# A four-image layer of state-space branches, attention and expert networks: row transfers stop beside one image's gates, one image's norm closes up, and a small table takes more of its operands from PSUM

## The chip, the cores and the metric

The kernel runs on one core of a Trainium2 chip. A core has five engines that each work through a queue of their own: TensorE (PE, matrix products), VectorE (DVE, elementwise work on tensors, scans and reductions), ScalarE (ACT, functions of one tensor), GpSimd (POOL, elementwise work and transfers by index) and SyncE (SP, transfers). An engine starts an instruction when the one before it is through and what it waits for has been signalled. Working memory is SBUF, with 128 partitions; PE writes its results to PSUM, a smaller memory of eight banks, which DVE and ACT read and write too. The metric is the device time of one launch in microseconds (us).

## The reference

The input x has the shape (4, 256, 32, 32): four images, 256 channels, 1024 positions. What is computed, cut to its order:

```python
x = x + conv_layer(_ln_c(x))          # the "metaformer" layer
t = tokens(x)                         # 4096 rows of 256 channels
t = t + experts(_ln_t(t))             # top 2 of 8 networks for each row

# conv_layer:
xn = layernorm(xs)                    # over channels
xm = mamba of each of 4 channel groups (xn) + skip * xn
g  = sigmoid(conv1d(conv1d(xm)))      # a gate of each group and position
xg = g * xm
R  = conv1d(depthwise3(xg)) + xg      # 3 taps along the positions, then channels mixed
xm2 = conv1d(depthwise3([xs, R])) + xs
out = mix([depthwise3(xm2), attention(xm2)])   # 8 heads, softmax over 1024 positions
... layernorm, gelu, 3 x 3 depthwise, layernorm, projection
```

The Mamba branch runs a recurrence of 16 states for each of 128 inner channels: `h = dA_t * h + dBu_t`, then `y_t = sum(h * C_t)`. The input of the layer is itself normalised over channels (`_ln_c`), so two layer norms follow one another; the kernel folds them into one mean, one variance and two roots. The expert layer sends each row to two of eight networks of width 1024.

## The kernel before

**Order.** The order of the instructions in every engine's queue is written out by hand: work is put into the queues in the order in which Python issues it (`tc.manual_schedule` over all five engines). Generators issue a few instructions and then yield a number of *ticks*. `beat()` (line 1571 and on) makes one tick: it steps every generator that is due, in the order in which they were started. The main loop, from about line 1605, puts one scan step into the queues and then calls `beat()`, so in a tick the scan's instructions come first and the rest follows.

**Scan.** An image b (0 to 3) has eight *parts*: four branches by two halves of 512 positions. A part has 16 scan steps. A step has, for 128x512 values each, the decay on ACT (line 732), the inflow on DVE (742), the recurrence as one scan instruction on DVE (753), the multiply with C on POOL (761, written dA<-hs,cs), the spread of B on PE (724) and the sum over states on PE (771). Around a part's start POOL also makes dt (682, 686), and at its end z (779).

**Beside and between the scans.** In the first half of image b's scan runs `convolutions(b-1)`: the gates (ACT 958 and 963, POOL 971) and the 3-tap depthwise convolutions `depthwise3` (the first tap on ACT, line 457; the two others on DVE, line 462). The products d4r<-xm come after them, with taps of the same function. After part 3 the scan's loop is interrupted for `attention(b-1)`: scores on PE (1140), exponentials on ACT (1150), pairs of them added on DVE (1200), the product with v on PE (1190). When its marker "attended" is set, the scan goes on with part 4, and whatever else is still running shares the ticks of the scan.

**The norm.** `normalised(b)` (from line 514) makes the normed input of image b. For image 2 it runs as an entry of its own, started together with attention of image 0: sums over the two channel chunks, centring, squares (POOL), column means (PE), the roots r1 and r2 (ACT, lines 419 and 420), then by chunk: xl = xn * r1 (POOL, 570), xn * r2 (DVE, 572), a transfer of xl to XL in DRAM, a scale and shift (POOL, 575), and `own_taps` (from 583): a first tap on ACT (586), two on DVE (593), a transfer to XD. The squares of image 2 are added up over the chunks into one operand (`one_chunk`), kept in the buffers of r1 and r2.

**Routing and row transfers.** When an image is finished, `sent_off` runs `experts.dispatch(b)`: it norms the rows, finds two experts for each, and writes each row into its expert's region of XS. That takes 16 transfers by index on POOL for each image (line 1975), each behind a small memset (1974). For image 0 two ticks lie between them. `dispatch(0)` runs in the scan of image 3, parts 0 and 1, beside `convolutions(2)`; it was started earlier, so in a tick its transfer is put in ahead of the gate's multiply.

**The expert tiles.** `tiles()` starts with the last part of the scan. It takes tiles of 256 rows, each of one expert. Which expert a tile has and where its rows begin is worked out in tables, one for each series of tiles: `series` calls `table` (line 2041 and on), some 22 DVE instructions on 128x8 or 128x64 values. The first table (series 0, in the last scan at about 1405 us) gets a PSUM bank, `first_table`, and keeps some of its operands there. The later tables are all in SBUF. After the scan of image 3 and its convolutions and attention, nearly all that is left is products of the expert tiles on PE (2364, 2397).

Of the kernel before, what the change touches and what calls it, by code (L numbers as in the profile page):

```python
# [11 lines left out]
ALU = mybir.AluOpType  # L12
AX = mybir.AxisListType

P = 128
# [4 lines left out]
HALF = 512  # L20
# [58 lines left out]
def network(  # L79
# [71 lines left out]
    with tc.tile_pool(name="w_conv", bufs=1) as wp, tc.tile_pool(  # L151
# [371 lines left out]
        def normalised(b):  # L523


            place_xn(b)
            xn = XN[b]

            def part(c, h):
                return xn[:, c, ds(LEFT + h * HALF, HALF)]  # L530

            yield 4

            def centre(h, mean):
                for c in range(NC2):
                    nc.vector.tensor_tensor(part(c, h), part(c, h), mean, ALU.subtract)

            r1, r2 = a4(f"r1_{b}"), a4(f"r2_{b}")
            one_chunk = b == 2
            if one_chunk:  # L540
                for h in range(2):
                    nc.gpsimd.tensor_tensor(r1[:, half(h)], part(0, h), part(1, h), ALU.add)
                yield 2
            yield from in_turn(
                range(2), lambda h: column_mean(
                    f"mean_{b}_{h}",
                    [r1[:, half(h)]] if one_chunk else [part(c, h) for c in range(NC2)],
                ),
                centre,
            )  # L550
            for h in range(2):
                if one_chunk:
                    sq = [v[:, half(h)] for v in (r1, r2)]
                else:
                    sq = [a2(f"sq_{b}_{h}_{c}") for c in range(NC2)]
                for c in range(NC2):
                    nc.gpsimd.tensor_tensor(sq[c], part(c, h), part(c, h), ALU.mult)
                if one_chunk:
                    nc.gpsimd.tensor_tensor(sq[0], sq[0], sq.pop(), ALU.add)
                    yield 1  # L560
                yield 1
                var = column_mean(f"var_{b}_{h}", sq)
                yield 2
                root(r1[:, half(h)], var, eps6)
                yield 1
                root(r2[:, half(h)], var, eps11, scale=1.0 + 1e-5)
                yield 1
            for c in range(NC2):
                xl = a4(f"xl_{b}_{c}")
                nc.gpsimd.tensor_tensor(xl, xn[:, c, LEFT:], r1, ALU.mult)  # L570
                yield 2
                nc.vector.tensor_tensor(xn[:, c, LEFT:], xn[:, c, LEFT:], r2, ALU.mult)
                yield 1
                nc.sync.dma_start(XL[b][:, c, :], xl)
                nc.gpsimd.tensor_scalar(
                    xn[:, c, LEFT:], xn[:, c, LEFT:], col("norm_w", c), col("norm_b", c),
                    ALU.mult, ALU.add,
                )
                yield 1
                if b in XD and b < B - 1:  # L580
                    yield from own_taps(b, c, xl)
# [330 lines left out]
        def convolutions(b):  # L912
# [54 lines left out]

            def gating():
                yield from in_turn(range(NC2), gate, keep)
                for c in range(NC2):  # L970
                    nc.gpsimd.tensor_tensor(
                        xm[:, c, 1 : N + 1], gs[c], xm[:, c, 1 : N + 1], ALU.mult
                    )
                    yield 1
                for c in range(NC2):
                    yield from depthwise3(d[1], c, xm, c, "rdw_w", c, col("rdw_b", c))

            def mixed(at, r):
                co, h = at
# [366 lines left out]
        def sent_off(b):  # L1346

            xc = XC.pop(b)
            beside = b < B - 2
            if b == B - 2:  # L1350
                yield 6

            def centre(h, mean):
                for c in range(NC2):
                    nc.vector.tensor_tensor(
                        xc[:, c, half(h)], xc[:, c, half(h)], mean, ALU.subtract
                    )

            pace(b, PACE["norm"])
            xr = a8(f"xr_{b}")  # L1360
            nc.sync.dma_start(xr, x[b].rearrange("(c p) n -> p c n", p=P))
            yield from in_turn(
                range(2),
                lambda h: column_mean(f"mean_{b}_{h}", [xc[:, c, half(h)] for c in range(NC2)]),
                centre,
            )
            yield from inverse_deviation(f"fin_{b}", xc, b == B - 1, b == 1)

            def residual(at, r):
                co, h = at  # L1370
                inner = xr[:, co, half(h)]
                if beside:
                    nc.scalar.activation(inner, r, AF.Identity, bias=prb[:, co : co + 1])
                else:
                    nc.vector.scalar_tensor_tensor(
                        inner, r, prb[:, co : co + 1], inner, ALU.add, ALU.add
                    )

            yield from in_turn(
                CO_H, lambda at: product(  # L1380
                    f"pr_{b}_{at[0]}_{at[1]}", projT_s, at[0],
                    [xc[:, ci, half(at[1])] for ci in range(NC2)],
                    xr[:, at[0], half(at[1])] if beside else None,
                ), residual,
            )
            T["projected", b] = True
            pace(b, PACE["routing"])
            for ticks in experts.dispatch(
                b, xr, act8.tile(experts.XR, F32, tag="a8", name=f"XR_{b}"), root,
                log_exp, lambda: T.get("exps"),  # L1390
            ):
                if experts.counted == b:
                    pace(b, PACE["rows"])
                yield ticks
            T["sent", b] = True
            pace(b, 1)
# [259 lines left out]
class Experts:  # L1656
# [155 lines left out]
    def s1(self, name):  # L1812
        return self.m0.tile([P, self.NT, 1], F32, tag=name, name=name)

    def dispatch(self, b, X1, XR, root, log_exp, recent):

        nc, tc, psum, m0, NT = self.nc, self.tc, self.psum, self.m0, self.NT
        s1, s3, all_e = self.s1, self.s3, self.all_e
# [152 lines left out]
        apart = self.apart  # L1971
        for j in range(2):
            for t in range(NT):
                nc.gpsimd.memset(apart, 0.0)
                ins = nc.gpsimd.indirect_dma_start(  # L1975
                    out=self.XS[:, :],
                    out_offset=bass.IndirectOffsetOnAxis(ap=to[:, j, t : t + 1], axis=0),
                    in_=XR[:, t, :], in_offset=None,
                )
                for other in self.sent + self.read:  # L1980
                    tc.declare_no_dep(ins.ins, other.ins, reason="no two share a row")
                self.sent.append(ins)
                if b == self.B - 2 and recent():
                    self.follow(ins, [recent()], "one after the other")
                if b == self.B - 1 and j == 0:
                    self.blank_end(t)
                yield 2 if b in (0, 2) or b == 1 and t % 2 else 1
# [53 lines left out]
    def table(self, temp, keep, name, n, ntile, which, done=None, kinds=NE, bank=None):  # L2041
# [16 lines left out]
        S = [P, n, kinds]  # L2058
        past = temp(f"past_{name}", S)
        nc.vector.tensor_tensor(past, which, ends.to_broadcast(S), ALU.is_ge)  # L2060
        if bank is None:
            inside = temp(f"inside_{name}", S)
        else:
            inside = bank[:, ds(3 * kinds, n * kinds)].rearrange("p (n e) -> p n e", e=kinds)
        nc.vector.tensor_tensor(inside, which, starts.to_broadcast(S), ALU.is_ge)
        nc.vector.tensor_tensor(inside, inside, past, ALU.subtract)
        expert = keep(f"expert_{name}", [P, n, 1])
        nc.vector.tensor_reduce(expert, past, AX.X, ALU.add)
        nc.vector.tensor_scalar(expert, expert, float(kinds - 1), None, ALU.min)
        if kinds > NE:  # L2070
            second = temp(f"second_{name}", [P, n, 1])
            nc.vector.tensor_scalar(
# [1 line left out]
            )  # L2074
            nc.vector.tensor_tensor(expert, expert, second, ALU.add)

        nc.vector.tensor_tensor(which, which, starts.to_broadcast(S), ALU.subtract)
        if done is not None:
            nc.vector.tensor_tensor(which, which, done.to_broadcast(S), ALU.add)
        nc.vector.tensor_scalar(  # L2080
            which, which, float(self.T), float(-self.SPARE), ALU.mult, ALU.add
        )
        for k in range(0, kinds, NE):
            nc.vector.tensor_tensor(
                which[:, :, k : k + NE], which[:, :, k : k + NE],
                self.region[:, 0:1, :].to_broadcast([P, n, NE]), ALU.add,
            )
        nc.vector.tensor_tensor(which, which, inside, ALU.mult)
        first = temp(f"first_{name}", [P, n, 1])
        nc.vector.tensor_reduce(first, which, AX.X, ALU.add)  # L2090
        table = self.m0.tile([P, 2, n], mybir.dt.int32, name=f"table_{name}")
        nc.vector.tensor_copy(table[:, 0, :], expert.rearrange("p n a -> p (n a)"))
        nc.vector.tensor_scalar(
# [458 lines left out]
```

## Time and profile before

| | us |
|---|---|
| three runs | 2158.35, 2160.07, 2161.26 |
| their median | 2160.07 |
| profiled execution | 2160.25 |
| its span, first to last instruction | 2158.5 |
| outside the span | 1.75 |
| PE busy | 1921.5 (89%) |
| DVE busy | 1539.0 (71%) |
| ACT busy | 1212.5 (56%) |
| POOL busy | 1052.9 (49%) |
| mean granted TensorE clock | 0.963 of full speed |

Stages of the profiled execution, in us from its start: scan of image 0 to about 260; first half of image 1's scan with convolutions of image 0 to about 435; attention of image 0 from 438 to 530; the second half of image 1's scan from there; attention of image 1 from about 793; the gates of image 2 and the last three row transfers of image 0 from 1084 to 1111; the first table from 1404 to 1412; the end of the last scan to 1437; expert tiles, with the rest of image 3, to the end.

A line of an engine's timeline reads: start in us, length in us, engine, line of the kernel, operation, output<-inputs by the program's names, the size of output and inputs, the number of instructions put together; in square brackets the idle time of the engine just before, and what ended it. Where one line stands for several instructions (x2 and more), its length covers them all.

### The profile page before, as it was taken

What the parts mean: (1) busy time and instruction counts of PE and PEld (TensorE: products, weight loads), DVE (VectorE), ACT (ScalarE), POOL (GpSimd) and SP (SyncE); (2) the same over time, 40 slices, a digit from 0 to 9 for tenths busy, and PEclk for the clock granted to TensorE, in tenths of its full rate; (3) what the DMA queues carried; (4) which work ended last, traced back from release to release, by engine and by line L of the source; (5) the groups of instructions that cost most, each with busy time, mean ns of one, the idle gap of its engine ahead of it and who ended that gap; (6) DMA issues with size and microseconds to landing.
All of it is one profiled execution on the core that took longest, in us unless ns stands there. A gap on an engine that the chain in (4) does not pass through costs nothing. (4 is left out here: it accounts for less than half of the span.)

```text
span 2158.5 us, 28179 instructions
## 1 busy us (share of the span) xinstructions
PE 1921.5 (89%) x8682; PEld 866.5 (40%) x8682; DVE 1539.0 (71%) x2253; ACT 1212.5 (56%) x2274; POOL 1052.9 (49%) x935
## 2 busy tenths in 40 slices
PE   6778778999887999988789999769999989999996
PEld 2112112322211232223123223226743768888885
DVE  3999999876999989789889898986265345221121
ACT  4665657678676667677466876625267423222221
POOL 0787887731887850376878016752031012422131
PEclk8888999999999999998999999999999999999998
DMA  3665544311454431053734203445230166877764
GB/s 99 152 161 127 125 122 102 90 41 50 105 117 122 94 85 40 17 133 98 187 87 108 80 6 98 109 162 146 81 92 23 47 198 172 233 230 189 212 185 131
DMA packets 157087, 251.40 MB, mean 116 GB/s; under 512 B 34740, under 2 KB 101332, under 8 KB 156664
## 3 DMA queue, kind: packets, MB, share of 16 engines
q1 hardware_dynamic: 136560, 223.47, 38.2%
q0 software_dynamic: 12720, 17.32, 4.1%
q10 hardware_dynamic: 7640, 8.65, 1.3%
q8 instruction: 72, 1.18, 0.2%
q14 instruction: 95, 0.78, 0.1%
HBM read 137.22 MB, written 36.62 MB: 81 GB/s over the span
## 5 line engine op out<-in xcount | busy, mean ns | idle before, releaser
L761 POOL TENSOR_TENSOR dA<-hs,cs 128x512 f32<-128x512 f32 x512 | 684.0, 1345 | 374.7 <-DVE hs L753 246.7
L732 ACT ACTIVATE dA<-dts,A 128x512 f32<-128x512 f32 x512 | 359.0, 718 | 152.6 <-DMA dts<-dt 68.8
L771 PE MATMUL yp<-dA,quads 128*32 128x512 f32 x1024 | 284.4, 631 | 87.5 <-POOL dA L761 72.8
L2382 POOL DMA_INDIRECT Y<-ys,dest x68 | 109.6, 1612 | 425.4 <-DVE ys L2375 418.4
L1150 ACT ACTIVATE e<-st 128x512 f32<-128x512 f32 x512 | 263.6, 605 | 86.8 <-PE st L1140 81.6
L2369 ACT ACTIVATE hs<-h,b 128x256 f32<-128x256 f32 (+1 forms) x256 | 110.2, 479 | 345.6 <-PE h L2364 241.3
L742 DVE TENSOR_TENSOR dBu<-dts,bs 128x512 f32<-128x512 f32 x384 | 259.8, 677 | 48.9 <-PE bs L724 14.5
L753 DVE TENSOR_TENSOR_SCAN hs<-dA,last,dBu 128x512 f32<-128x512 f32 x192 | 243.7, 1269 | 2.9 <-PE yp L771 1.1
L2397 PE MATMUL y<-w,hs 128*128 128x256 f32 (+1 forms) x1088 | 243.3, 382 | 0.7 <-issue 0.4
L2364 PE MATMUL h<-xT,w 128*128 128x256 f32 (+1 forms) x1024 | 239.6, 390 | 0.8 <-DVE xT L2327 0.8
L753 DVE TENSOR_TENSOR_SCAN hs<-dA,dBu 128x512 f32<-128x512 f32 x192 | 231.9, 1208 | 1.9 <-PE av L1162 1.3
L1200 DVE TENSOR_TENSOR e<-e,e 128x512 f32<-128x512 f32 x256 | 171.0, 729 | 74.7 <-ACT e L1150 45.7
L2397 PEld LDWEIGHTS y<-w,hs 128*128 128x128 f32 (+1 forms) x1088 | 197.2, 188 | 37.7 <-issue 9.8
L2364 PEld LDWEIGHTS h<-xT,w 128*128 128x128 f32 x1024 | 195.3, 192 | 41.9 <-issue 8.3
L2327 DVE COPY xT<-xp 128x512 f32<-128x512 f32 (+1 forms) x36 | 23.3, 647 | 246.2 <-PE xp L2323 245.9
L724 PE MATMUL bs<-u,xpwT_s 128*32 128x512 f32 x1024 | 157.4, 651 | 39.7 <-DVE hs L753 15.0
L1140 PE MATMUL st<-qk 32*128 32x512 f32 x1024 | 174.4, 638 | 1.3 <-DVE hs L753 1.2
L771 PEld LDWEIGHTS yp<-dA,quads 128*32 128x32 f32 x1024 | 50.6, 112 | 297.7 <-POOL dA L761 196.4
L1190 PE MATMUL av<-e,v 128*32 128x512 f32 x1024 | 138.6, 604 | 0.0
L1975 POOL DMA_INDIRECT XS<-XR,to x64 | 65.6, 1025 | 92.3 <-ACT e L1150 53.9
L1140 PEld LDWEIGHTS st<-qk 32*128 32x128 f32 x1024 | 60.1, 183 | 115.7 <-issue 87.1
L742 DVE TENSOR_TENSOR bs<-dts,bs 128x512 f32<-128x512 f32 x128 | 86.2, 673 | 0.9 <-DMA dts<-dt 0.9
(374 smaller groups left out, 2637.3 us busy)
## 6 DMA issues: line engine op xcount, KB each, us to landing
dts<-dt SPq DMA_DIRECT2D x512, 128.0 KB
w<-in_W_dram SPq DMA_DIRECT2D x124, 512.0 KB
cs<-cd SPq DMA_DIRECT2D x512, 64.0 KB
xs<-XS SPq DMA_DIRECT2D x32, 260.0 KB
xd<-xn SPq DMA_DIRECT2D x64, 128.0 KB
xn<-in_x_dram SPq DMA_DIRECT2D x8, 512.0 KB
XL<-xl SPq DMA_DIRECT2D x8, 512.0 KB
xl<-XL SPq DMA_DIRECT2D x4, 1024.0 KB
```

The source lines that it names most:

```text
L724: nc.tensor.matmul(bs[r], xpwT_s[:, n, s : s + 1].to_broadcast([P, 32]), T[b, n, "u"][:, half(h)], start=True, stop=True,)
L732: nc.scalar.activation(dA, T[b, n, h, "dts", g][:, 0, :], AF.Exp, scale=A[:, g, n, q : q + 1])
L742: nc.vector.tensor_tensor(dBu, T[b, n, h, "dts", g][:, 1, :], T[b, n, h, "bs", q], ALU.mult)
L753: nc.vector.tensor_tensor_scan(hs, T[b, n, h, "dA", i], dBu, 0.0 if h == 0 else last, ALU.mult, ALU.add)
L761: nc.gpsimd.tensor_tensor(dA, hs, T[b, n, h, "cs", q], ALU.mult)
L771: nc.tensor.matmul(T[b, n, h, "yp"][ts(g, 32)], quads, T[b, n, h, "dA", q * GD + g], start=False, stop=(q == GS - 1),)
L1140: nc.tensor.matmul(sts[i], k[r, ts(kt, P)], q[r, half(h)], start=True, stop=not shifted)
L1150: ins = nc.scalar.activation(es[i], sts[i], AF.Exp, scale=1.0 / HD**0.5)
L1190: nc.tensor.matmul(accs[0][ts(i, HD)], v8[:, kt, ts(4 * g + i, HD)], es[i], start=(kt == 0), stop=(kt == NK - 1),)
L1200: nc.vector.tensor_tensor(first[i], first[i], es[i], ALU.add)
L2364: nc.tensor.matmul(hp[:, i, :], w1(c, k0 + i), xT[:, c, :], start=(c == 0), stop=(c == NC2 - 1))
L2397: nc.tensor.matmul(yp[ts(k % parts, n), ts(t % 2, C)], hidden(k)[:, ds(t * P, n)], w2(k), start=(k < parts), stop=(k >= NHC - parts),)
```

## The change

The change has three parts.

- `normalised`: the squares and the two roots become small functions. For image 2 alone the order is new: squares of half 0; a tick later squares of half 1 and the variance of half 0; then a root in each tick, with the variance of half 1 in the tick of its first root. That makes 6 ticks, where each half had 6 before. The other images keep their order.
- `convolutions` and `dispatch`: a marker `gating` is set from the first gate multiply until the two depthwise convolutions behind the gates are through (2 + 2 × 3 = 8 ticks), in images 0 to 2. `dispatch` yields a tick at a time while it is set, ahead of each transfer. Only `dispatch(0)` beside the gates of image 2 meets the marker.
- `table`: with a bank, the count of each tile's expert (`last`), the first row (`first`), the comparison with starts (`within`) and the products (`tell`) are in PSUM; `inside`, which was there, is in SBUF. Only the first table has a bank.

```diff
@@ normalised(b)
-            for h in range(2):
+            def squares(h):
                 if one_chunk:
                     sq = [v[:, half(h)] for v in (r1, r2)]
...
                 if one_chunk:
                     nc.gpsimd.tensor_tensor(sq[0], sq[0], sq.pop(), ALU.add)
-                    yield 1
-                yield 1
-                var = column_mean(f"var_{b}_{h}", sq)
-                yield 2
+                return sq
+
+            def roots(h, var):
                 root(r1[:, half(h)], var, eps6)
                 yield 1
                 root(r2[:, half(h)], var, eps11, scale=1.0 + 1e-5)
                 yield 1
+
+            if one_chunk:
+                sq = squares(0)
+                yield 1
+                sq, var = squares(1), column_mean(f"var_{b}_0", sq)
+                yield 1
+                yield from roots(0, var)
+                yield from roots(1, column_mean(f"var_{b}_1", sq))
+            else:
...
@@ convolutions(b), gating()
                 yield from in_turn(range(NC2), gate, keep)
+                T["gating",] = beside
                 for c in range(NC2):
...
                     yield from depthwise3(d[1], c, xm, c, "rdw_w", c, col("rdw_b", c))
+                T["gating",] = False
@@ dispatch
         for j in range(2):
             for t in range(NT):
+                while busy():
+                    yield 1
                 nc.gpsimd.memset(apart, 0.0)
@@ table
+        inside = temp(f"inside_{name}", S)
         if bank is None:
-            inside = temp(f"inside_{name}", S)
+            within, tell = inside, which
         else:
-            inside = bank[:, ds(3 * kinds, n * kinds)].rearrange("p (n e) -> p n e", e=kinds)
-        nc.vector.tensor_tensor(inside, which, starts.to_broadcast(S), ALU.is_ge)
-        nc.vector.tensor_tensor(inside, inside, past, ALU.subtract)
+            at = iter(range(3 * kinds + 2 * n, HALF, n * kinds))
+            within, tell = (
+                bank[:, ds(next(at), n * kinds)].rearrange("p (n e) -> p n e", e=kinds)
+                for _ in range(2)
+            )
+        nc.vector.tensor_tensor(within, which, starts.to_broadcast(S), ALU.is_ge)
+        nc.vector.tensor_tensor(inside, within, past, ALU.subtract)
         expert = keep(f"expert_{name}", [P, n, 1])
-        nc.vector.tensor_reduce(expert, past, AX.X, ALU.add)
-        nc.vector.tensor_scalar(expert, expert, float(kinds - 1), None, ALU.min)
+        if bank is None:
+            last, first = expert, temp(f"first_{name}", [P, n, 1])
+        else:
+            last, first = (
+                bank[:, ds(3 * kinds + k * n, n)].rearrange("p (n a) -> p n a", a=1)
+                for k in range(2)
+            )
+        nc.vector.tensor_reduce(last, past, AX.X, ALU.add)
+        nc.vector.tensor_scalar(expert, last, float(kinds - 1), None, ALU.min)
...
-        nc.vector.tensor_tensor(which, which, starts.to_broadcast(S), ALU.subtract)
+        nc.vector.tensor_tensor(tell, which, starts.to_broadcast(S), ALU.subtract)
...
-        nc.vector.tensor_reduce(first, which, AX.X, ALU.add)
+        nc.vector.tensor_reduce(first, tell, AX.X, ALU.add)
```

More of the change, by code (lines that the diff above doesn't have):

```diff
@@ L567, in normalised @@
                 yield 1
+            if one_chunk:
[6 more added lines that the diff above has]
+            else:
+                for h in range(2):
+                    sq = squares(h)
+                    yield 1
+                    var = column_mean(f"var_{b}_{h}", sq)
+                    yield 2
+                    yield from roots(h, var)
             for c in range(NC2):
@@ L1389, in sent_off @@
                 b, xr, act8.tile(experts.XR, F32, tag="a8", name=f"XR_{b}"), root,
-                log_exp, lambda: T.get("exps"),
+                log_exp, lambda: T.get("exps"), lambda: T.get(("gating",)),
             ):
@@ L1813, in s1, with dispatch @@
         return self.m0.tile([P, self.NT, 1], F32, tag=name, name=name)
-    def dispatch(self, b, X1, XR, root, log_exp, recent):
+    def dispatch(self, b, X1, XR, root, log_exp, recent, busy):
         nc, tc, psum, m0, NT = self.nc, self.tc, self.psum, self.m0, self.NT
@@ L1973, in dispatch @@
             for t in range(NT):
+                while busy():
+                    yield 1
                 nc.gpsimd.memset(apart, 0.0)
@@ L2075, in table @@
             nc.vector.tensor_tensor(expert, expert, second, ALU.add)
-        nc.vector.tensor_tensor(which, which, starts.to_broadcast(S), ALU.subtract)
+        nc.vector.tensor_tensor(tell, which, starts.to_broadcast(S), ALU.subtract)
         if done is not None:
-            nc.vector.tensor_tensor(which, which, done.to_broadcast(S), ALU.add)
+            nc.vector.tensor_tensor(tell, tell, done.to_broadcast(S), ALU.add)
         nc.vector.tensor_scalar(
-            which, which, float(self.T), float(-self.SPARE), ALU.mult, ALU.add
+            tell, tell, float(self.T), float(-self.SPARE), ALU.mult, ALU.add
         )
@@ L2084, in table @@
             nc.vector.tensor_tensor(
-                which[:, :, k : k + NE], which[:, :, k : k + NE],
+                tell[:, :, k : k + NE], tell[:, :, k : k + NE],
                 self.region[:, 0:1, :].to_broadcast([P, n, NE]), ALU.add,
             )
-        nc.vector.tensor_tensor(which, which, inside, ALU.mult)
-        first = temp(f"first_{name}", [P, n, 1])
-        nc.vector.tensor_reduce(first, which, AX.X, ALU.add)
+        nc.vector.tensor_tensor(tell, tell, inside, ALU.mult)
+        nc.vector.tensor_reduce(first, tell, AX.X, ALU.add)
         table = self.m0.tile([P, 2, n], mybir.dt.int32, name=f"table_{name}")
```

## The prediction

> **What bounds the kernel now.** I read the page's slices first, then sums over stretches, then each engine's instructions in order around the three edits, and last the waits in the tail.
>
> The slices: forty rows of tenths. The change acts in three places, and each has its own limit.
>
> ```profile
> PE   6778778999887999988789999769999989999996
> ...
> DVE  3999999876999989789889898986265345221121
> ...
> POOL 0787887731887850376878016752031012422131
> ```
>
> VectorE (DVE) stands at 9 in the scan of image 0, falls to 6 to 7 in slices 8 to 9 (attention of image 0) while TensorE is at 9, and rises again; from slice 27 on TensorE is the full engine. Sums over stretches (from:to, length, busy PE, weight loads, DVE, ACT, POOL, granted clock, DMA share, GB/s) sharpen that:
>
> ```profile
> 438.00:530.00 92.00, 92.00 (x632) 26.52 (x624) 62.68 (x80) 74.01 (x145) 18.32 (x14) 1.00 0.10 33
> ...
> 550.00:750.00 200.00, 167.22 (x605) 44.87 (x598) 193.69 (x215) 139.49 (x249) 166.03 (x124) 0.97 0.49 116
> ...
> 1413.50:1437.40 23.90, 14.09 (x33) 2.20 (x34) 19.79 (x25) 3.63 (x7) 22.30 (x27) 0.93 0.53 185
> 1450.00:1700.00 250.00, 246.88 (x1264) 135.30 (x1263) 121.09 (x223) 137.76 (x250) 41.60 (x52) 1.00 0.27 79
> ```
>
> Attention of image 0 (438 to 530) is bound by TensorE: 92.00 of 92.00. The scan behind it is bound by DVE, 193.69 of 200 (97%), so a microsecond taken off DVE there is one off the time. At the end of the last scan POOL leads (22.30 of 23.90), and from 1450 TensorE leads with 246.88 of 250: what comes earlier before it moves the end by as much, since that tail has next to nothing to absorb it.
>
> **Edit A, norm of image 2.** Before, each half takes 6 ticks (squares, 2 ticks, variance, 2, root, root), 12 in all; after, the sequence takes 6. All behind it comes 6 ticks earlier. No instruction is added. Its start lies in the first attention tick, its end spills into the scan. DVE in order there:
>
> ```profile
> 531.74 1.20 DVE L572 TENSOR_TENSOR xn<-xn,r 128x1024 f32<-128x1024 f32 x1
> 533.66 0.70 DVE L742 TENSOR_TENSOR dBu<-dts,bs 128x512 f32<-128x512 f32 x1 [0.72 <-ACT e L1150]
> 535.62 1.22 DVE L753 TENSOR_TENSOR_SCAN hs<-dA,dBu 128x512 f32<-128x512 f32 x1 [1.25 <-PE av L1162]
> ...
> 544.84 1.43 DVE L593 SCALAR_TENSOR_TENSOR taps<-xl,V,taps 128x1023 f32<-128x1023 f32 x1
> ...
> 547.91 1.25 DVE L593 SCALAR_TENSOR_TENSOR taps<-xl,V,taps 128x1023 f32<-128x1023 f32 x1
> ```
>
> The two L593 taps lie in unbroken DVE work: 1.43 + 1.25 = 2.68 us come off. The L572 multiply (1.20) is already covered, as DVE waits 0.72 and 1.25 right behind it for others. Also moved with no gain: the POOL scale L575 (2.67 us), the ACT tap L586 (about 1.24), the XL and XD stores on SP's queue, earlier by 6 ticks and with nobody waiting. They cost nothing while attention has room (POOL 18.32 of 92, DVE 62.68); without that cover A's gain would be gone. What it can cost: the four roots now fall into consecutive ticks, each 1.31 us of ACT (L419 0.68 + L420 0.63), which also makes the exponentials (L1150) that PE's next product waits for. ACT's room is 92 − 74.01 = 18 us, over some 30 ticks 0.6 each. Bounds: 0 (absorbed; the same roots were there before, in two pairs) to 4 × (1.31 − 0.6) = +2.8. I take +0.5, nearer the lower end, because only the pairing is new. A: −2.7 + 0.5 = **−2.2** (−3.9, if the multiply counted too, to +0.1).
>
> **Edit B, row transfers of image 0.** Sixteen transfers (L1974, L1975), two ticks apart, pass POOL's queue beside the gates of image 2. The flag stands for 8 ticks from the first gate multiply, so thirteen are out already and three, at 1089.26, 1097.78 and 1106.58, go 8 ticks back. No semaphore wait is added; POOL's z, dt and dA (L779, L682, L686, L761) just come ahead of them in its queue. On DVE, taps of L462:
>
> ```profile
> 1093.22 5.45 DVE L462 SCALAR_TENSOR_TENSOR d<-xm,V,d 128x1024 f32<-128x1024 f32 x1 [4.02 <-ACT d L457]
> ...
> 1100.38 2.79 DVE L462 SCALAR_TENSOR_TENSOR d<-xm,V,d 128x1024 f32<-128x1024 f32 x1
> ```
>
> On POOL beside it:
>
> ```profile
> 1090.30 2.37 POOL L971 TENSOR_TENSOR xm<-g,xm 128x1024 f32<-128x1024 f32 x1
> 1092.61 1.28 POOL L779 TENSOR_TENSOR z<-y,z 128x512 f32<-128x512 f32 x1
> 1093.85 1.27 POOL L761 TENSOR_TENSOR dA<-hs,cs 128x512 f32<-128x512 f32 x1
> 1095.09 1.27 POOL L682 TENSOR_TENSOR dt<-low,over 128x512 f32<-128x512 f32 x1
> 1096.33 1.26 POOL L761 TENSOR_TENSOR dA<-hs,cs 128x512 f32<-128x512 f32 x1
> ```
>
> The tap needs 1.25 (L462: median 1.280, shortest 1.252). It starts at 1093.22 and ends at 1098.67, when POOL's unbroken row ends. The same stretch of images 0 and 1 has no transfers and so shows the time without them. From the start of the first tap to the end of the fourth: image 0 345.63 to 358.65, image 1 703.39 to 716.41, 13.02 us both (taps of 1.88, 1.73 to 1.74, 1.25, 1.25); image 2 1093.22 to 1110.87, 17.65. From ACT's g (L963) it is 22.45, 22.44 and 27.07. So B takes off **4.6** here. The 4.02 us wait for ACT d stays: image 1 has 4.01 of it.
>
> [...]
>
> Where the three transfers go, POOL's slack per tick is 0.44 to 0.56 beside a 1.27 dA (1112 to 1122), while a transfer with its memset and gap takes about 1.27. Two ticks' slack does not quite hold it, so POOL falls behind by about 0.3 each, and the third transfer is in the tick of the first d4r tap (1121.45). Who waits behind it on POOL: dA, then PE's sums, then DVE's taps if they meet POOL's unbroken run again. Bounds: −0.6 (nothing met, and a dA leaves a gap used by DVE) to +4.2 per tap (5.45 − 1.25). I take one meeting like the second tap: 2.79 + 1.26 against 2 × 1.26 is 1.5, less part of the 0.63 us for which DVE waits next: **+1.3**. The XS rows are read first by the expert tiles, over 250 us later. B: **−3.3** (−5 to +1.5).
>
> **Edit C, first table.** The count `last`, `first`, `within` and `tell` go to PSUM; `inside` goes to SBUF. About 22 small instructions stay as many.
>
> ```profile
> 1406.81 1.62 DVE L2069 TENSOR_SCALAR expert<-expert 128x8 f32<-128x8 f32 x1
> ...
> 1408.56 0.23 DVE L2080 TENSOR_SCALAR which<-which 128x64 f32<-128x64 f32 x1
> ...
> 1409.55 1.38 DVE L2092 CAST table<-expert 128x8 int32<-128x8 f32 x1
> ```
>
> Without POOL beside it (second table, 1725 us) L2069 takes 0.17, L2092 0.22. With `last` in PSUM, L2069 is to be 0.17: −1.45. The cast still reads `expert` from SBUF; it comes 1.45 earlier, at another point of POOL's run (6.51 of 7.60 busy): from −1.16 (free) to +1.15 (blocked by twice as much). I take −0.95: it would begin at about 1408.10, and POOL's dA of 1407.10 (1.26) ends at 1408.36, with a short pause ahead of a transfer behind it, the pause in which L2069 came through. C: **−2.4** (−0.3 to −2.6). [...]
>
> Is the gain carried to the end? POOL waits there for DVE:
>
> ```profile
> POOL dA L761 <- DVE hs L753: 2.6, 1, 2.6
> ```
>
> That wait, just ahead of POOL's unbroken run from 1413.54, has room for the whole 2.4, and behind it POOL and then PE are full. Without that wait C would be worth nothing.
>
> **Sum.** −2.2 − 3.3 − 2.4 = −7.9 us. The profiled execution took 2160.25 us (span 2158.5 and 1.75 outside it, unchanged): 2152.35. The runs' median of 2160.07 is 0.18 lower: **2152.2 us**.
>
> **Rivals.**
> 1. *Given back* (0.17). The postponed transfers block d4r taps for as much as B gained (−4.6 + 4.2), and the roots eat A (−0.5): −0.9 − 2.4 = −3.3, 2156.8; nothing to tell from no change. For it: POOL's 0.5 us of slack. Against it: the third tap, beginning at 1106.66 beside the transfer of 1106.58, took 1.25.
> [...]
> 3. *Slower* (0.09): the transfers, at 1112 to 1122, leave POOL without a pause and each of the four d4r taps is blocked as the first gate tap was: 4 × 4.2 = 16.8 against 4.6 + 2.2 + 2.4 = 9.2, so +7.6, 2167.7. It turns slower only above 13.5 us of loss (9.2 + 4.3), more than three taps. For it: nothing has to be added to what 1093.22 shows. Against it: POOL pauses within two ticks of the last transfer, so the third and fourth taps are free.
> 4. *The schedule falls otherwise* (0.04): A's shift makes exponentials late all through attention, the 24 ticks left × ACT's 0.6 us of room lost = 14.4 against 7.9: +6.5, 2166.6.
>
> The sum's case has 0.60. **Chances.** Measurement can tell 0.2%, 4.3 us, from none. Faster (below 2155.8): the sum's case, save its upper edge, and a part of 1 and 2: 0.68. Same: 0.20; slower 0.12. The range: low end with all good bounds, −3.9 − 5 − 2.6 = −11.5, 2148.5, a little under it 2147.5; upper end takes in 1 and 2 and B's bad bound (+0.1 + 1.5 − 0.3 = +1.3) to 2162. Sum's case alone: 2148.5 to 2155.5.
>
> **What would show it.** A: no L593 tap of image 2 left in the scan, the resumed scan 2.7 us nearer to attention's end; attention as long as before. B: taps of 1.88, 1.73, 1.25, 1.25 beside the gates and 13.0 us over the four; d4r taps of L462 no longer than 2.8. C: L2069 at 0.17, POOL's wait for hs near 0.3 instead of 2.6. Wrong, if one of the d4r taps is at 5, if the first gate tap is above 3 with no transfer near, or if the tail starts as late as now.

## The result, and the profile after

The changed kernel takes 2154.5 us (median of 13 runs, 2147.9 to 2159.8), the kernel before, run beside it, 2161.88 (13 runs, 2158.35 to 2165.96). The ratio is 0.9963, 95% interval 0.9955 to 0.997: 8.0 us less (0.0037 × 2161.88), interval 6.5 to 9.7; the two medians by themselves lie 7.4 apart. Run again on another occasion it was 0.997 (0.9962 to 0.9979), 6.5 us less. The profiled execution took 2155.93 us, span 2154.2, which is 4.3 less than the span before.

The slices of the page after; PE and DVE are as full as before over the whole (89% and 71%), and no work has passed from one engine to another.

```profile
PE   6888778999987999988789999769999989999996
...
DVE  3999999877999988789889898986265355321211
...
POOL 0787887732787850376887016652031012422221
```

Edit A. Sums over attention of image 0, with the columns as before: PE is still never idle, and DVE and ACT have taken in the rest of the norm (DVE 62.68 before, 68.07 now).

```profile
438.00:530.00 92.00, 92.00 (x629) 26.48 (x625) 68.07 (x85) 76.16 (x148) 20.73 (x14) 1.00 0.12 42
```

The taps of image 2's norm (line 607 now), from the list by tile (ns of the shortest, median and longest, then the first and last start): all four start before 523 us, where two stood at 544.84 and 547.91.

```profile
L607 DVE SCALAR_TENSOR_TENSOR taps<-xl,V,taps x4: 1272/1284/2522, 502.4 to 522.6; 128x1023 f32<-128x1023 f32 x4
```

Edit B. DVE's timeline beside the gates and at the first d4r tap:

```profile
1092.43 1.87 DVE L462 SCALAR_TENSOR_TENSOR d<-xm,V,d 128x1024 f32<-128x1024 f32 x1 [4.01 <-ACT d L457]
...
1096.01 1.75 DVE L462 SCALAR_TENSOR_TENSOR d<-xm,V,d 128x1024 f32<-128x1024 f32 x1
...
1116.02 2.94 DVE L462 SCALAR_TENSOR_TENSOR d4r<-xm,V,d4r 128x1024 f32<-128x1024 f32 x1
```

The gate taps take 1.87 and 1.75 instead of 5.45 and 2.79. The first d4r tap, which took 1.26, takes 2.94. POOL beside it, with the second and third of the postponed transfers:

```profile
1114.31 1.01 POOL L1993 DMA_INDIRECT XS<-XR,to  x1 [0.17 <-issue]
1115.36 2.51 POOL L775 TENSOR_TENSOR dA<-hs,cs 128x512 f32<-128x512 f32 x2
1117.81 0.10 POOL L1992 MEMSET apart<- 128x1 f32 x1
1118.07 1.78 POOL L1993 DMA_INDIRECT XS<-XR,to  x1 [0.16 <-issue]
1120.90 2.15 POOL L775 TENSOR_TENSOR dA<-hs,cs 128x512 f32<-128x512 f32 x1 [1.06 <-DVE hs L767]
```

The tap asks at 1116.02 and ends at 1118.96; its 1.25 us of work can begin at about 1117.7, when the second of the two dA ends. POOL's own wait of 1.06 behind is for the scan that the tap held up. In the view of waits (us in total, times, longest), PE then stands for POOL in the stretch 1120 to 1130, 0.6 us before and 3.1 now:

```profile
PE yp L771 <- POOL dA L761: 0.6, 1, 0.6
```

```profile
PE yp L785 <- POOL dA L775: 3.1, 1, 3.1
```

Edit C. The first table on DVE:

```profile
1405.38 0.17 DVE L2099 TENSOR_SCALAR expert<-first_table 128x8 f32<-128x8 f32 x1
...
1406.79 0.16 DVE L2121 CAST table<-expert 128x8 int32<-128x8 f32 x1
...
1407.18 0.17 DVE L2235 TENSOR_SCALAR taken<-taken 128x8 f32<-128x8 f32 x1
1407.39 1.89 DVE L2236 TENSOR_TENSOR taken<-taken,ntile 128x8 f32<-128x8 f32 x1
1409.32 0.17 DVE L2239 COPY done<-taken 128x8 f32<-128x8 f32 x1
```

The two long ones are short, as meant: 1.62 to 0.17, and 1.38 to 0.16. But `taken<-taken,ntile`, a minimum of two SBUF operands that took 0.17 before (first line below), now takes 1.89, beside these two of POOL (second and third line):

```profile
1411.30 0.17 DVE L2207 TENSOR_TENSOR taken<-taken,ntile 128x8 f32<-128x8 f32 x1
```

```profile
1406.93 1.01 POOL L1993 DMA_INDIRECT XS<-XR,to  x1 [0.16 <-issue]
1407.97 1.28 POOL L775 TENSOR_TENSOR dA<-hs,cs 128x512 f32<-128x512 f32 x1
```

The view of waits at the end of the scan says what is left of the gain: POOL stood 2.6 us for DVE's scan before, and still stands 2.1.

```profile
POOL dA L775 <- DVE hs L767: 2.1, 1, 2.1
```

### The profile page after: what moved, and what is told of

The parts are those of the page before. It is cut to its first block, busy times and chain, and to the rows that moved or that the text cites. A ratio compares the mean times of both kernels' runs of the same rounds, so it can differ in the third digit from the quotient of the medians.

```text
span 2154.2 us, 28178 instructions
## 1 busy us (share of the span) xinstructions
PE 1923.2 (89%) x8682; PEld 866.3 (40%) x8682; DVE 1535.4 (71%) x2253; ACT 1212.9 (56%) x2274; POOL 1051.9 (49%) x935
```

## How the stages compare

The three edits lie far apart in time. In the stages of this table that an edit does not touch, the traces agree to 0.1 us, most to 0.03, except where PE's matmuls ran slowly (the last section): that moves the third row, in which no edit acts, and part of the sixth. With this care each edit can be read as the time between the starts of the same two instructions in two traces (in us, from the starts in the traces' timelines):

| from, to | before | after | after, again | A only | B only | C only | later stop | taken in PSUM |
|---|---|---|---|---|---|---|---|---|
| attention of image 0, first to last product st listed | 88.74 | 88.31 | 88.30 | 88.32 | 88.71 | 88.73 | 88.32 | 88.30 |
| the 16 scan steps behind it | 38.14 | 36.32 | 36.32 | 36.33 | 38.13 | 38.13 | 36.33 | 36.32 |
| scan steps 288 to 304, before attention of image 1 | 32.29 | 33.95 | 33.91 | 33.94 | 33.88 | 33.93 | 30.69 | 33.93 |
| gates of image 2 (steps 404 to 409) | 23.47 | 18.85 | 18.85 | 23.47 | 18.86 | 23.47 | 18.85 | 18.85 |
| first d4r taps (409 to 418) | 20.13 | 21.08 | 21.07 | 20.13 | 21.08 | 20.03 | 19.39 | 21.08 |
| behind them (418 to 440) | 40.53 | 42.39 | 42.34 | 40.53 | 41.18 | 40.53 | 40.97 | 42.37 |
| first table (499 to 504) | 16.22 | 15.65 | 15.64 | 16.21 | 16.20 | 15.87 | 15.87 | 14.06 |

The step numbers count the 512 scan instructions on DVE. "First to last listed" is from the first st product of image 0 to the 241st.

## The experiments

### Each edit alone

```diff
 # A only, B only, C only: the kernel before, with
+ the new order of normalised(2)              # A
+ T["gating",] and `while busy(): yield 1`    # B
+ last, first, within, tell in the bank       # C
```

> The kernel before with the closer norm of image 2 alone. Theory: the two L593 taps of image 2 leave the scan, so scan steps behind 569 us come about 1.8 to 2.7 us earlier than before; the time is 2.2 us below the kernel before. In the trace of the changed kernel 1.65 us of this were handed back at 753.7, where DVE waited 2.82 us for PE instead of 1.17, after PE had stood idle for 2.10 us and then ran matmuls of 512 columns in 1.06 us instead of 0.59. If that belongs to the edit, it is at the same place here; if it is the clock's own timing, it is there or not as it falls, and somewhere else in other kernels. Rival: attention hands the gain back (its 30 ticks longer by 2 us or more), time as before.

Measured: ratio to the kernel before 1.0002 (0.9991 to 1.0012). In the stages A is clean: −0.42 in attention and −1.81 in the scan steps behind, 2.23 together, and attention is no longer. The whole run does not show it: its interval, from 1.9 us less to 2.6 more, ends just short of the 2.2 that were expected. The step at 753.7 is there too (33.94 in the third row), but also in B only (33.88) and C only (33.93), which have no A: it is not A's.

> The kernel before with the stop of the row transfers alone. Theory: taps beside the gates 1.88, 1.75, 1.25, 1.25 instead of 5.45, 2.79, 1.25, 1.25, 4.6 us less; the first d4r tap 2.9 instead of 1.26 behind the postponed transfers, about 1.0 back; a PE wait of about 3 us for POOL's dA near 1123, and slow matmuls behind it, up to 1.9 more back: the time 1.8 to 3.6 us below the kernel before. [...]

Measured: 0.999 (0.998 to 1.0001), 2.2 us less, upper end at none. The gates go from 23.47 to 18.86 (−4.61), the first d4r taps from 20.13 to 21.08 (+0.95), what follows from 40.53 to 41.18 (+0.65): −3.0.

> The kernel before with the first table's operands in PSUM alone. Theory: L2069's operation 0.17 instead of 1.62, the cast of L2092 0.2 to 0.4 instead of 1.38; POOL's wait for hs at 1413.5 about 0.3 instead of 2.65, expert tiles 2.3 us earlier; time 2.4 us below the kernel before. Rival: POOL is late anyway, the tiles start within 0.5 us of where they did, time as before.

Measured: 1.0005 (0.9993 to 1.0016). By stage 16.22 to 15.87: −0.35, not −2.4. POOL's wait for the scan is 2.30 where 2.65 stood. The rival was nearer: the tiles do not start earlier, though not because POOL is late but because DVE meets another wait three instructions on. Here it is not the minimum that takes it up but the operation just ahead of it, a maximum with zero that has one SBUF operand:

```profile
1412.17 1.96 DVE L2217 TENSOR_SCALAR taken<-taken 128x8 f32<-128x8 f32 x1
```

### A later stop

```diff
                 for c in range(NC2):
                     yield from depthwise3(d[1], c, xm, c, "rdw_w", c, col("rdw_b", c))
-                T["gating",] = False
...
             for c in range(NC2):
                 for ticks in depthwise3(d[1], c, xm, c, "fdw_w", NC2 + c, ...):
                     next(gated, None)
                     yield ticks
+            T["gating",] = False
```

> The changed kernel with the stop of image 0's row transfers held until image 2's d4r taps are through too. Theory: a postponed transfer costs only where a DVE tap meets POOL's unbroken run, so all four d4r taps take 1.25 (the first 2.94 in the changed kernel), PE does not wait 3 us for dA near 1123; 1 to 2.9 us below the changed kernel, 9 to 11 us below the kernel before. Rival, that the three transfers cost the same wherever they are put (POOL's time itself is the price): as the changed kernel, 8 us below the kernel before.

Measured: 0.9977 (0.9968 to 0.9986), 5.0 us below the kernel before. All four d4r taps take 1.25; the stage is 19.39 instead of 21.08, and the next 40.97 instead of 42.39: −3.1 against the changed kernel in this trace. Only the first part, −1.69, is firm: with the same stop the next stage took 43.76 and 40.96 in two more traces (below). The transfers, now at 1136 to 1146, cost at most 0.44 us there (40.97 against 40.53 before), so the price is mainly the meeting with a tap and not POOL's time. The whole time does not show it: 5.0 less than before is no better than the changed kernel's 6.5 to 8.0. Its trace lost 1.7 us at about 890 us and 3.0 at about 975 in slow PE stretches that the trace of the changed kernel doesn't have (granted clock 0.89 over 885 to 900 us and 0.87 over 970 to 990, where the changed kernel has 1.00).

### Plain work in the transfers' old places

```diff
                 while busy():
+                    if b == 0 and len(self.stood) < 6:
+                        if len(self.stood) % 2 == 0:
+                            nc.gpsimd.memset(apart, 0.0)
+                            stand = XR.rearrange("p t c -> p (t c)")[:, 0:412]
+                            nc.gpsimd.tensor_tensor(stand, stand, stand, ALU.mult)
+                        self.stood.append(1)
                     yield 1
```

> The changed kernel, with a plain multiply of about 1.0 us (128x412, over rows of image 0 that are sent already) and the memset in each of the three places beside the gates from which the transfers were taken; the transfers themselves come 8 ticks later as in the changed kernel. Theory that the transfer itself makes DVE wait on: taps beside the gates 1.9, 1.75, 1.25, 1.25. Rival that POOL's run without a pause does it, whatever is in it: 5.4 and 2.8 again, and 4.6 us of the gain gone.

Measured: 0.9994 (0.9985 to 1.0003), the gain is gone. The gates take 24.00 us, more than the 23.47 of before. DVE's first tap, and POOL from just before it until it stands still:

```profile
1088.33 7.08 DVE L462 SCALAR_TENSOR_TENSOR d<-xm,V,d 128x1024 f32<-128x1024 f32 x1 [4.02 <-ACT d L457]
```

```profile
1087.28 1.27 POOL L793 TENSOR_TENSOR z<-y,z 128x512 f32<-128x512 f32 x1
1088.51 1.27 POOL L775 TENSOR_TENSOR dA<-hs,cs 128x512 f32<-128x512 f32 x1
1089.75 1.26 POOL L696 TENSOR_TENSOR dt<-low,over 128x512 f32<-128x512 f32 x1
1090.98 1.26 POOL L775 TENSOR_TENSOR dA<-hs,cs 128x512 f32<-128x512 f32 x1
1092.18 0.09 POOL L1994 MEMSET apart<- 128x1 f32 x1
1092.24 0.86 POOL L1996 TENSOR_TENSOR XR<-XR 128x412 f32<-128x412 f32 x1
1093.07 1.26 POOL L700 TENSOR_TENSOR dt<-dt,u 128x512 f32<-128x512 f32 x1
1097.28 2.22 POOL L775 TENSOR_TENSOR dA<-hs,cs 128x512 f32<-128x512 f32 x1 [2.95 <-DVE hs L767]
```

There is no transfer here, and the tap waits longer, 7.08: through seven POOL instructions without a pause, until the last of them ends at 1094.33. So the long wait does not need the transfer: plain work in its place brings it too, as the rival has it, though not with the rival's numbers (the second tap took 1.25 and not 2.8). The transfers were even the milder filling: each has some 0.16 us of standing still ahead of it ("issue" in the brackets). The tap of the kernel before began its 1.25 us of work at about 1097.4 (1098.67 − 1.25), at the end of the multiply ahead of such a pause:

```profile
1096.33 1.26 POOL L761 TENSOR_TENSOR dA<-hs,cs 128x512 f32<-128x512 f32 x1
1097.53 0.09 POOL L1974 MEMSET apart<- 128x1 f32 x1
1097.78 1.78 POOL L1975 DMA_INDIRECT XS<-XR,to  x1 [0.15 <-issue]
```

But POOL's run without a pause is not by itself what shuts DVE out. The third tap of this same trace was let in when the third of the plain multiplies ended, with POOL's dA directly behind it, which then had to wait:

```profile
1101.86 1.69 DVE L462 SCALAR_TENSOR_TENSOR d<-xm,V,d 128x1024 f32<-128x1024 f32 x1
```

```profile
1101.59 0.88 POOL L1996 TENSOR_TENSOR XR<-XR 128x412 f32<-128x412 f32 x1
1102.42 2.25 POOL L775 TENSOR_TENSOR dA<-hs,cs 128x512 f32<-128x512 f32 x1
```

What POOL has in the two control images, and lacks in the long waits of 5.45 and 7.08 us, is a moment of standing still ahead of z, 1.03 and 0.80 us, seen in the trace before:

```profile
343.92 1.28 POOL L779 TENSOR_TENSOR z<-y,z 128x512 f32<-128x512 f32 x1 [1.03 <-ACT y L778]
...
701.68 1.28 POOL L779 TENSOR_TENSOR z<-y,z 128x512 f32<-128x512 f32 x1 [0.80 <-ACT y L778]
```

The changed kernel has 0.16 us there; the kernel before beside image 2's gates, and the stand-in, have none. In the short cases the tap also asks while dA is in progress, in these two long ones while z is in progress. Which of the two matters is not shown.

### The tiles taken, in PSUM too

```diff
-        taken = temp(f"taken_{s}", [P, 1, NE])
+        taken = temp(f"taken_{s}", [P, 1, NE]) if bank is None else (
+            bank[:, ds(HALF - NE, NE)].rearrange("p (a e) -> p a e", a=1)
+        )
```

> The changed kernel with the tiles taken by series 0 in the same PSUM bank too. In the changed kernel the minimum of two SBUF operands (taken<-taken,ntile) takes 1.89 instead of 0.17 and gives back most of what the count and the cast won. Theory: it takes 0.17 here, the tiles start 1.7 us earlier than in the changed kernel, 7 to 8 us below the kernel before by stages. Rival: the next DVE instruction (the copy to done, or the inflow) takes up the wait; as the changed kernel.

```profile
1407.50 0.17 DVE L2237 TENSOR_SCALAR first_table<-first_table 128x8 f32<-128x8 f32 x1
1407.71 0.17 DVE L2238 TENSOR_TENSOR first_table<-first_table,ntile 128x8 f32<-128x8 f32 x1
1407.92 0.17 DVE L2241 COPY done<-first_table 128x8 f32<-128x8 f32 x1
```

Measured: 0.9949 (0.9933 to 0.9964). The minimum takes 0.17, the copy behind it too, and POOL's wait for hs falls to 0.53. The table's stage is 14.06 (16.22 before, 15.65 changed): now C takes off 2.2 us, of the 2.4 that were forecast for it, and the changed kernel had reached 0.6. Once more:

> The changed kernel with the tiles taken in PSUM, once more, for its interval and the places of PE's slow steps. By stages 7 us below the kernel before (5.3 of the three edits and 1.6 of the taken tiles); by its first, wide interval 11. The stage of the first table 14.06 again (16.22 before, 15.65 changed).

Measured: 0.9961 (0.9948 to 0.9973), the stage at 14.08.

### The two together, and the changed kernel once more

> The changed kernel with the later stop and with the tiles taken in PSUM, both. If the two add up: 2 (stop) and 1.7 (taken) below the changed kernel, some 9 us below the kernel before. Rival: once one of them is done POOL or PE is late in the other place too, no better than either alone.

Measured: 0.9948 (0.9928 to 0.9969); stages 19.39 and 14.23. The stage behind the d4r taps took 43.76 here, more than the changed kernel's 42.39.

> The changed kernel with the later stop and the tiles taken in PSUM, once more. By stages 9 us below the kernel before, 2 below the one with the tiles alone; if the later stop's 2 us are eaten by PE's slow steps after an idle, the same as that one. The d4r stretch 19.4 again (20.1 before, 21.1 changed), the table's 14.1 to 14.2.

Measured: 0.9965 (0.995 to 0.998); 19.39 and 14.23 again, and 40.96 behind the taps. In their own stages both gains are there each time; one kernel's two traces differ by 2.8 us in the stage between. They also show edit A's 16 scan steps at 37.54 and 38.01 instead of 36.32, with PE at half clock for 3.4 us from 531 and from 529 us. By the whole time the two edits together are some 7.6 to 11.2 us below the kernel before, the tiles taken in PSUM alone 8.4 to 11.0, and the changed kernel 6.5 to 8.0; the intervals overlap, so that either beats the changed kernel is likely by the stages but not shown by the times.

> The changed kernel once more, beside the kernels it is compared with. By the stages of the traces so far (attention of image 0 to 569 us −2.24, gates −4.6, d4r stretch +1.6 to +2.8, table −0.4 to −0.6) 5 to 6 us below the kernel before; by its first measurement 8. The PE steps after an idle of over 2 us fall differently here from the first trace of the same kernel if the clock's timing, not the edit, placed them: the handed-back 1.65 us at 753.7 may be there or not.

Measured: 0.997 (0.9962 to 0.9979), 6.5 us less. The handed-back step before attention of image 1 is there again (33.91).

## Why the prediction was right, point by point

**The sum.** Forecast −7.9 us, 2152.2; measured 2154.5, and as a ratio −8.0 and −6.5. The total fits better than its terms do: in the trace their stages come to −4.6 (below), and with edit C's term mostly gone, that the total still fits is in part luck.

**Edit A**, −2.2: it is −2.25 (−0.43 in attention, −1.82 behind). The mechanism is the forecast one; the exact fit is luck, because the terms missed to both sides. The two taps gave 1.35 and 1.19 where 2.68 was reckoned; 0.72 came back within 20 us in two short waits, the longer 0.52 us for ACT. The +0.5 for late exponentials did not come: attention was 0.4 shorter. The L572 multiply was covered, as stated (DVE's wait for ACT behind it grew from 0.72 to 1.84).

**Edit B**, −3.3: −4.62 at the gates against −4.6 from the two control images. The first d4r tap gave 0.95 back (2.94 instead of 1.26, less a DVE wait of 0.63 us for PE that vanished, is 1.05), against +1.3. What the sum lacked is what came next: PE waited 3.1 us for POOL's dA, and its next matmuls then ran slowly (granted clock over 1120 to 1136 us 1.00 before, 0.68 in the changed kernel, 0.79 in B only): +1.86 and +1.81 in two traces of the changed kernel, +0.65 in B only. With that B is −1.8 to −3.0. The reason was half right: the prediction took the two control images to show the time without the transfers. They differ also in POOL's standing still ahead of z (1.03 and 0.80 us there, none beside image 2's gates in the kernel before), and a plain multiply in place of the transfers does as much harm. The prediction's worst case for B, +1.5, does not follow from its own terms either: one tap at +4.2 gives −0.4, two give +3.8.

**What the long taps wait for.** The taps of 5.45, 2.94 and 7.08 us were held up over several POOL instructions (four, two and seven). Their last 1.25 us begin at 1097.42, 1117.71 and 1094.16, by their ends, and the last POOL multiply ahead of a pause, if only of 0.16 us, ends at 1097.59, 1117.87 and 1094.33. In other places DVE was let in at the first end of a POOL instruction (the tap of 1.87 us at 1092.43, that of 1.69 in the stand-in). What decides between the two isn't settled here.

**Edit C**, −2.4: this step failed. Its two terms came (−1.45 as forecast, and −1.22 where −0.95 was taken), but the sum stopped at them. It did not ask which of the remaining SBUF operations would now stand where the cast had stood: `taken<-taken,ntile` reads two SBUF operands, comes at 1407.39 while POOL runs through a transfer and a dA to 1409.25, and takes 1.89. Net −0.57, and −0.35 alone, where the maximum ahead of it takes 1.96. With that operand in PSUM too it is −2.2. The wait was not one of the instruction, but of the moment: it was 1.62 us at the count's minimum before, 1.96 at the tiles' maximum in C only and 1.89 at the tiles' minimum here, each with an operand in SBUF. The move to PSUM cost nothing in itself in the first table's 64-element multiply and add: 232 ns before, in SBUF, and 232 after, in PSUM.

**The rivals.** "Given back" described B's loss in kind but was too large in size, and none of them had C's; "slower" had four taps blocked, where one was. That B would bring nothing fell with the −4.6 at the gates, and "the schedule falls otherwise" with attention 0.4 shorter.

**What stays open.** By stage the three edits come to −0.43 − 1.82 − 4.62 + 0.95 + 1.86 − 0.57 = −4.6 in the trace of the changed kernel, while the runs say −8.0 and −6.5. That its span is 4.3 shorter is not a check of this sum: at the last scan step the changed kernel's trace is only 2.2 us ahead, as slow PE steps gave back part of the gain (+1.66 in the third row alone), and the other 2.2 come behind it, where no edit acts. And the edits alone, by their whole times, come to less than the three together: +0.4, −2.2 and +1.1 us, −0.7 in sum, each uncertain by about 2. One trace is one execution, and runs of the same kernel differ by some 12 us. The last section shows one reason; that it explains the difference between stages and runs is not shown.

## What to carry to other kernels

Moving to PSUM the operands of one instruction that is held up beside another engine's run may only hand its wait on (here 1.62 us at one instruction, then 1.89 at a later one): list every instruction behind it whose operands stay in SBUF, because a later one can inherit the wait. When work is moved off a crowded place, ask what stands at its new place; here a tap, 8 ticks on. And when a stage's repeat elsewhere in the trace serves as a control, check that the two differ in one thing only; a stand-in of about the same length tells whether the thing suspected is needed at all.

## What the runs showed of the hardware

**PE's slow steps.** After PE had stood idle for 2.10 us, its matmuls of 512 columns in the trace after started 0.85 us apart (at 736.35) where they had been 0.43 apart (at 733.23). The same idle of 2.10 us, ending at 736 to 739 us, was followed by no slow matmul in the kernel with the later stop, by 2.9 us of them in the trace before, and by 6.7 in the trace after. The granted clock stood at half for 3.4 us in the trace before (740.7 to 744.1) and for 6.8 in the trace after (736.6 to 743.4), and at full over 720 to 760 with the later stop. Sums over 735 to 745, before and after; the granted clock is the third value from the end:

```profile
735.00:745.00 10.00, 7.90 (x26) 1.83 (x24) 10.00 (x12) 6.20 (x16) 9.26 (x7) 0.83 0.11 31
```

```profile
735.00:745.00 10.00, 8.65 (x23) 1.96 (x24) 10.00 (x13) 5.35 (x13) 9.74 (x8) 0.66 0.11 34
```

The stage took 30.69, 32.29 and 33.95 us in these three: steps of 1.6. Half clock for 3.4 us costs PE an estimated 1.7 us of work (half of 3.4) and for 6.8 us 3.4, which is about the size of these steps. All stretches at half clock in the traces before and after, up to the one that runs to the end, lasted 3.4 us or a multiple of it (3.4 to 17.1).

Whether the slow steps come depends on the execution. The two traces of the kernel with both further edits took 33.93 and 30.69 us in this stage, and in the 100 scan steps behind it (304 to 404), where no edit acts, 323.87 and 328.48. So one trace is good for the length of a stage without a PE idle ahead of it, not for the sum over the kernel. The gain or loss of an edit that sits before such an idle can be lost to a step or two of 1.6, or be made larger by them.

**DVE beside POOL's runs.** A DVE instruction was kept for up to 5.8 us (7.08 − 1.25) by a POOL run of seven instructions, one that used 0.17 us for up to 1.8 (1.96 − 0.17). The long waits at taps (5.45, 2.94 and 7.08 us) ended with the last POOL multiply ahead of a pause, even one of 0.16 us, but a run without a pause did not always bring one (1.69 and 1.87 us).
